# Four-layer graph network on one core: four-head attention weights that hold the target exponential, with key tiles added pairwise by DMA, and residual adds and moments on VectorE and ScalarE

## The chip, the cores and the metric

The kernel runs on one core of a Trainium2 chip. The metric is the device time of one execution in microseconds (us). Three executions of the kernel before took 4344.05 to 4347.82 us, with a median of 4347.32 us.

## What is computed

The input `x` holds 16 graphs of 1024 nodes with 256 features, and `adj` is one 1024 x 1024 adjacency matrix for all of them. Four layers follow one another, each with a residual around it: `x = x + layer(relu(layernorm(x)))`. Everything is float32.

- Layers 0 and 1 are graph attention with one head. `h = inp W`, the score of query i and key j is `leaky_relu(s_i + t_j)`, where `s = h a1` and `t = h a2`; scores off the graph are masked, softmax runs over j, and the result is `attention h`, followed by relu (layer 0) or elu (layer 1).
- Layer 2 is dot-product attention with 8 heads of 32 features, masked with `adj`, followed by a layer norm, a feed-forward block of two 256 x 256 products with relu, and a second layer norm.
- Layer 3 is graph attention with 4 heads of 64 features and elu.

The core of layer 3 in the reference:

```python
ei = jnp.einsum('bhnd,hd->bhn', Wh, a1)
ej = jnp.einsum('bhnd,hd->bhn', Wh, a2)
e = ei[:, :, :, None] + ej[:, :, None, :]
e = jnp.where(e > 0, e, ALPHA * e)
e = jnp.where(adj[None, None] > 0, e, MASK_VAL)
att = jax.nn.softmax(e, axis=-1)
h = jnp.einsum('bhij,bhjd->bhid', att, Wh)
```

The kernel never forms e. Up to factors of i, which softmax cancels, `exp(leaky_relu(s_i + t_j))` is `max(r_i, e_j) * z_j` with `r_i = exp((alpha-1) s_i)`, `e_j = exp((1-alpha) t_j)` and `z_j = exp(alpha t_j)`. The last one, `z_j`, is called the target exponential here.

## The kernel before

**Stages and order.** A stage is one layer of one graph. The list `order` interleaves them: in the middle of the run the cycle is layer 2 of graph b, layer 1 of graph b+1, layer 3 of graph b, layer 0 of graph b+2. A stage's keys lie on the 128 partitions in 8 tiles j of 128 keys; queries lie along the free dimension.

**The planner.** Every piece of work is an `op` with an engine, a cost, a rank and the ops it waits for; buffers are `Hold`s in `Ring`s that an op takes and others end. At build time `forward` plays all ops against these costs and writes the instructions of each engine in that order. The stored string `RANKS` gives each op's due time, so the order on all engines is fixed before the run. VectorE and GpSimd ops that both read two tiles are marked `tiles`; the planner doesn't let them overlap.

**Layer 3** (`pair_item`, `pair_weights`, `pair_out`). For each of two head pairs hp and each key tile j, VectorE makes a tile p of 128 keys x 2 heads x 1024 queries (1 MB) with two instructions of line 1391: `max(r, e) * mask`, where r is a broadcast row of 1024 queries that comes by DMA through DRAM (line 1281), e is a per-key scalar and mask is uint8. Two key tiles make a step. TensorE multiplies them with the values v (line 1425: 16 matmul calls with 32 columns of weights each, 32 instructions in the trace), and then with the target exponential, spread over 32 columns, which gives the softmax sums (line 1449: 8 calls, 16 instructions in the trace). The values v themselves were multiplied by the target exponential by VectorE when they left the projection (lines 1183 and 1202). After 4 steps the accumulators are copied out by ScalarE (line 1440), transposed, divided by the sums, and added into x.

**Layer 2** (`dot_item`). For each half n of the queries, each group g of 4 heads and each key tile j: scores on TensorE (line 1545), exp on ScalarE (line 1559), mask on VectorE (line 1567), product with the values (line 1576). For two key tiles in turn, GpSimd issues a DMA that adds the odd tile of weights into the even one (line 1593, 1 MB), and TensorE sums only the added tile, with the constant 0/1 matrix `pick` (line 1605).

**Layers 0 and 1** (`gat_item`). VectorE makes the weights (line 1318), TensorE multiplies (line 1335), `gat_out` scales and adds the residual.

**Way in.** `way_in` normalises a node tile for the next layer: `stats_of` runs bn_stats and bn_aggr on VectorE (lines 1030, 1031) and the power -1/2 on GpSimd (lines 1034, 1035). Residual adds of layer 0 (line 1361) and of layer 2 (line 1738), and the add after the attention of layer 2 (line 1658), run on GpSimd.

**Buffers.** The ring `m` has 11 buffers of 1 MB for p, pe, q, k, y and the broadcast rows of layer 3; PSUM has three double banks (`u`), of which a score op takes two.

Of the kernel before, what the change touches and what calls it, by code (L numbers as in the profile page):

```python
# [28 lines left out]
U8 = mybir.dt.uint8  # L29
# [18 lines left out]
    "##,#M5#IA#&O#H2#2l#M)#'c#Q(#H#$6p#MC#GP##q##c#%-#$X##s##0##U#$0#$,##P##X##Y##1#$-##{#$)#$]#$M#%I#$j#$N#%E#%K#%Y"  # L48
    "##%#%O#%}#&Y#&d#&l#&s#';#'B##W##9#oB##N##B#oP##Z##?##>##[##D#ny##a$7g##`##r##l#$##$$#$8#$*##u##z#$6#$=##}#$(#$;"
    "##b#$V$8-##_##y$8,##d##A$7y##g##o#$'#$u##2#$9#$7#$K#%*##*#$H##]#$.##3#$A##t##v#$E#$F#,;##x##6#$5$%$##'#Q.##T#K9"  # L50
    "#K.#(,#%W#'`#'U#$n#)s#'k#%U#(`##^#%7#$&#$%#$1#$2#$C#$G#$I#$L##<#$?#$[#$4##f#%@#%L#&2#$<#$Q##j#81##w#%D#%Z#%`#Nz"
    "#$Z#$`####$r#&1#%f#%k#$Y#$k#%4#>9#%A#%5#%r#%&#%M#${#%=#&##xD#%{#'u#%a#'q#(:#%z#'t#$i##h#$+#$d#$_#$h#$s#$e#$@#`+"
    "#%?#$>#&B#&%#,R#&Z#[=#%;#$O#$v##i##H#'H#%g#%J#%[#%0#%/#%,#&M$D{#$x#%>#%N#%h#b8$?s#&0#(3#&+#&.#%y#%u#&($4Z#&&#&6"
    "#%b#&$#&)#&'$B+#&_#))#&:#%p#Du#;z#<%#%V##n$H^#$b#$p$3b#$^#T>$3P#$m#%1##(#%T##O#%|##R#$}$GF##-#$U##4##8##K#%.##$"
    "##M#%:#$y#$t#$q##I#$z#%<#$W#%)#%8#=M#%6#%+##/##&##@#$g#$a#%w#-%#-##%R$&s##5$=J#%H#%]#3Q#%i#,V#/+#&5#$l#&h#:-#CG"
    "#:=#%d#$S#$|#%2#%c#%j#%m#&,#%t#$J#$w#%x$?=#%C#)*#%F#%B#%l#$o#&-#(U#%Q#'2#+6#%o#&/#0,$'e#'G#h`##p#0'#%^#&7$Gw##k"
    "#%v$Hv#&F$Ha#&N#'-#&A#&Q#&V#&S#lN#&m#&4#'3#'/#b##':#%q#&a#&*#(l#&w#&{#&z#&9#&<$Hw#%S#(R#y$#(S#'6#&;#&?#&^#lO#&G"
    "#Y}#'X#'0#&W#&I#%X#)D#(?#'+#R0#&[#&L#&P#'J#(+#&H#'1#&R#&|#',#'@#&p#'Q#'r#&k#'Y#&f#'C#(f#'.#'L#(8#(=#'N#&U#;v#;l"
    "$-[#&K#&=#&b#&E#&g#&j#&t#''#%s#&i#&o#(y#'9#(;#6F#(<#&n#'$#'8$H'#'a#'y$4|#'5#&]#')#'s#&}$Bt#'^$7k#'l#'?#'<$C2#'h"
    "#'K#'}#<K#%$#'o##.#(6##C#'W#%(#(%##e#'E#'4#'S#'m#'R#'I#(5#'w#'(#'>#'x#jJ#&y$=Z#<J$:z#'F#'O#'7#%G#{)#&v#'z#)V#>U"  # L60
    "#'n#'_#%n#(&#'p#?/#(0#'M#(.#&J#(/#'j#&`#rr#_c#(F#8j#(q#Mm#(M#Mo#(d#Mn#'&#'%#(##'Z#{g#(*#)a#&8##:#(2#(N#(E#/V#)I"
    "#(B#(A#(C#(4#)]$+r#,e#)M#([#i&#((#()#,t#i'#w/#)c#(t#I2#(J#(Y#]h#(K#(V#)F#(_#Ms#(u#KE$Ea#)-#(c#N+#)S#IC#)b#)`#)g"
    "#)U#(i#)d#*(#8?#(m#(|#).#jZ#)1#(a#)$#LT#)##(g#)u#jQ#)n#)0#*R#(k#)8#)@#)C#(j#(]#({#(@#)R#']#)E#(Z#(n#'{#'A#(^#)T"
    "#)>#)G#(P#)&#)5#)v#*&#'P#(G#(X#)y#'D#)L#*q#);#Lj#'|#(9#*3#*$#(D#*,#)K$I0#(O$I@$,q#*##)B#)i#*;#(H#*+#*4#+H#*E#)J"
    "#+L#*9#)A#s}#**#(1#+@#)O#)x#*7#*P#/`#*a#*A#*Z#*8#VE#)?#*D#*0#*y#*6#-0#)N#*_#*k#+k#*s#*C#*^#b($$C#)=#*c#)t#*v#J2"
    "#*[#(w#*w#+U#*I#*i#zG#'v$>>#B=#*]#*g$J:#,h$%D#W5#*n#*M#+<#*|$B<#++#*O#WG#+/#*J#.'#+G$J;#+M#+?#*f#z}#*t#a)#*r$?%"
    "#+A#+8#*j#*u$3:#*d#*p#+d#+a#*S#,U#+C#)+#*-#+`#)}#+&#*K#/?#+R#CO#+O#+P#*}#+[#*'$*M#+^#+S#-[#+X#+c#),#0>#)4#)9#,$"
    "#'*#,v#+N#,r#,W#-<#,N#[S#,x#,O#-:#+D#-A#-G#,B#,d#-(#,j#-;#,L#--#+z#-C#,z#'[#-6#,i#-D#/b#[@#-I#.^#-a$EU#.J#.%$;%"
    "#-}#+b#-j#g)#.:#.)$9j#.7#.?#+B#+F#-H#+(#,&#R+#,D#,%#^1#+#$(u$%|#+)#(Q#-Z#,|#)Y#Lh#*>#2n#+g#+J#*1#cw#)X#,T#+T#,g"
    "#.&#,y#,l#+3#*)#,Z#+e#(-#+>#cj#,'#(L#-2#,5#,)#g`#,6#,:#,4#+}#,##C(#,Q#($$1`#+Z#,9#,X$5H#*L#)W$1_#,Y#-s#,0#+o#,b"  # L70
    "#|5#*B#,}#+r#,s#,?#,@#,>#+u#,n#,8$5J$=r#,K#+]#-Q#+n#.,#-?#.;#,J#+j#+p$5Q#)P#.<$5K#,f#+i#,M#,G#)%#+{#,1#,H#rc#+l"
    "$5P#,3#,S#zA#):#,I$Ab#,c#,/$En#.4$02#*F#,`#,u#,7#-9#+V#-e#,*#-c#.=#-v#-^#-@#-o#-Y#+q#-3#-K#-n#-p#.I#+f#.H#JZ#kE"
    "#,m#.P#.U#,k#.T#-|#.o#/(#k3#.V#.Y#-r#.b#.d#/3#,[#.*#-U#.t#.g#.s#.]#/1#-E#.R#.w#.W#.v#.n#,P#+.#-L#,+#-h#ho#/f#/P"
    "#-5#.k#/O#,]#,-#/Q#0r#/K#/)#/^#8/#-t#8M#-x#-w#/W#-l#)f#(s#)l#)[#*l#+4#)m#*N#*m#)o#+'#%'#)e$<.#*.#)w#*:#*<$Eg$,p"
    "#it#*`#*T#(x#*b#*U#(z$GW#)r#*/#*%#)z#(I#*Y#){#,(#)Q#)|#+I#*e#(>#)Z#*V#*X#)<#*x#*h#W6#+%#+7#`p#+*#+5#`s#+-#+9#^*"
    "#+0$%f#*=#.N#-'#-&#-)#+y#-,#-1#,a#-/#-4#-7#-]#z6#-J$;&#,_#-f#-d#.D#-$#-P#&C$;5#+:#.6#+=#-`#-i#-q#.3#J[#/d#0y#0U"
    "#.M#rQ#B3#.@#-B#,o#.K#,{#0n#._#?V#-g#-z#/t#,.#.9#.e#.G#/Y#.E#.h#/>#-k#./#.L#-F#.+#.8#.A#-X#.C#/0#-=#-{#/'#8-#.["
# [281 lines left out]
    "$Fz$IH$J-$HT$Ib$79#Ul$I?$J5$I+$G|$Iu#hA$EL$Hp$HW$H?$GV$I/$.{$HD#`j$Ig$H_$H:$78#<0#V>$J.$Hs$Ho$Du$HG#GJ$I.$Hu$H|"  # L359
    "#1Z$3G$Hf$HS#_;$HL$Hg$IW#('#y'#<E#xi$I_$J*#M{$J#$I1$J1$GR$I|#<x$II$GO$I($IS#WD$IX$Ia$IV$I]$IB#UX#UW$IT$@<$Im$I="  # L360
    "#q^$IG$IU$IQ$Id$IO#^r$IM#>M$Iz$HI$2d$CB#>e$Iy#yW$It$I}#p4#TS$J?$0R#pU$IZ$Ie$Ij$HN$I:$J@$Hq$Hm$Ih$IP$IL$Ip$I$#:["
    "$I,$IN#5e$I'$If$IY#Y&$Hy#m_$J6#%P$J%#jY$Il#k;#al$J8#wr$I{$J'$J9$Ir$I>"
)


# [1585 lines left out]
```

## Time and profile before

| what | us |
|---|---|
| three executions, median | 4347.32 |
| the profiled execution, whole | 4346.76 |
| its span, first to last instruction | 4344.9 |
| TensorE matmuls busy in it | 4143.8 (95%) |
| VectorE busy | 3368.5 (78%) |
| ScalarE busy | 2004.2 (46%) |
| GpSimd busy | 1408.4 (32%) |
| queue of the adding DMAs, share of 16 DMA engines | 30.7% |

In the profile, PE is TensorE, PEld its weight loads, DVE is VectorE, ACT is ScalarE, POOL is GpSimd and SP issues most DMAs. A row of a group gives line, engine, operation, output and inputs, count, busy time and mean duration of one, and then the idle time just before, with what ended it. The busy time of a group can be less than count times mean, since consecutive instructions overlap a little.

### The profile page before, as it was taken

Reading aid. Unit: us, or ns where it says so; the run is one execution under the profiler, and the core shown is the slowest. Engines: PE = TensorE matmul, PEld = TensorE weight load, DVE = VectorE, ACT = ScalarE, POOL = GpSimd, SP = SyncE. Lnnn points to the kernel's source line nnn. Section 1 sums busy time; section 2 is a strip of 40 time slices with the busy share of each in tenths; the row PEclk is TensorE's granted clock in tenths of the full one; section 3 lists DMA queues with packets and bytes.
Section 4 is the critical chain, followed back from the end, with each engine's and each line's share of the span. In section 5 each row is a group of like instructions: output and inputs, shape, how many; then the busy total and the mean of one; then the engine's idle time right before and its main releaser. Section 6 shows DMA issues by size and latency. Waiting matters only on the chain. (4 is left out here: it accounts for less than half of the span.)

```text
span 4344.9 us, 66664 instructions
## 1 busy us (share of the span) xinstructions
PE 4143.8 (95%) x25993; PEld 2175.8 (50%) x25993; DVE 3368.5 (78%) x5836; ACT 2004.2 (46%) x3083; POOL 1408.4 (32%) x2281
## 2 busy tenths in 40 slices
PE   8999999998999999999999999998999999899988
PEld 7735264553645535455354554535545355464433
DVE  7578877878777788777878778777787877858788
ACT  4462635435354453634536354363543635455442
POOL 3323242423324233242322424224242241434231
PEclk9999999999999999999999999999999999999999
DMA  3061805317053170531606235162350713435261
GB/s 111 17 142 32 169 27 117 69 50 155 25 119 79 40 148 26 129 71 46 140 26 141 59 75 111 37 130 59 74 112 33 150 42 89 96 75 111 64 122 41
DMA packets 96451, 364.29 MB, mean 84 GB/s; under 512 B 10376, under 2 KB 45568, under 8 KB 63360
## 3 DMA queue, kind: packets, MB, share of 16 engines
q0 software_dynamic: 36864, 268.45, 30.7%
q1 hardware_dynamic: 58848, 90.98, 6.2%
q8 instruction: 206, 3.38, 0.3%
q14 instruction: 117, 0.96, 0.1%
q10 hardware_dynamic: 416, 0.52, 0.0%
HBM read 74.32 MB, written 17.17 MB: 21 GB/s over the span
## 5 line engine op out<-in xcount | busy, mean ns | idle before, releaser
L1567 DVE TENSOR_TENSOR pe<-pe,mask 128x1024 f32<-128x1024 f32 x1024 | 1206.9, 1233 | 190.5 <-ACT pe L1559 188.3
L1559 ACT ACTIVATE pe<-sc 128x1024 f32<-128x1024 f32 x1024 | 995.4, 1023 | 369.7 <-PE sc L1545 313.8
L1335 PE MATMUL av<-v,p 128*128 128x257 f32 x4096 | 966.8, 387 | 8.5 <-DVE p L1318 6.1
L1335 PEld LDWEIGHTS av<-v,p 128*128 128x128 f32 x4096 | 771.1, 192 | 202.2 <-issue 62.0
L1391 DVE SCALAR_TENSOR_TENSOR p<-r,e,mask 128x1024 f32<-128x1024 f32 x512 | 621.9, 1274 | 95.7 <-DMA r<-kept 85.8
L1545 PE MATMUL sc<-qT,kT 32*128 32x512 f32 x4096 | 626.3, 645 | 2.5 <-ACT pe L1559 2.5
L1035 POOL TENSOR_TENSOR rstd<-rstd,minus_half 128x1 f32<-128x1 f32 x768 | 565.5, 736 | 64.0
L1576 PE MATMUL acc<-pe,v 128*32 128x512 f32 x4096 | 543.0, 605 | 6.1 <-DVE pe L1567 4.7
L1593 POOL DMA_DIRECT2D pe<-pe x256 | 225.6, 888 | 976.8 <-PE acc L1576 669.5
L1034 POOL TENSOR_SCALAR rstd<-stats 128x1 f32<-128x1 f32 x768 | 281.8, 367 | 789.5 <-DVE stats L1031 765.3
L1425 PE MATMUL acc<-p,v 128*32 128x512 f32 x4096 | 465.9, 593 | 0.0
L1605 PE MATMUL sums<-pe,pick 128*32 128x512 f32 x2048 | 294.6, 637 | 127.2 <-DMA pe<-pe 126.4
L1545 PEld LDWEIGHTS sc<-qT,kT 32*128 32x128 f32 x4096 | 192.6, 184 | 388.8 <-issue 184.4
L1061 PE MATMUL pm<-l_wx,hT 128*128 128x259 f32 (+1 forms) x1536 | 369.5, 389 | 2.4 <-ACT hT L1057 1.4
L1318 DVE SCALAR_TENSOR_TENSOR p<-r,e,mask 128x512 f32<-128x512 f32 x512 | 359.2, 755 | 6.8 <-DMA r<-kept 6.4
L1061 PEld LDWEIGHTS pm<-l_wx,hT 128*128 128x128 f32 x1536 | 287.4, 191 | 73.1 <-ACT hT L1057 12.8
L1361 POOL TENSOR_TENSOR x<-x,o 128x256 f32<-128x256 f32 x128 | 100.6, 787 | 570.4 <-ACT o L1357 570.1
L1425 PEld LDWEIGHTS acc<-p,v 128*32 128x32 f32 x4096 | 132.1, 110 | 293.1 <-issue 277.4
L1576 PEld LDWEIGHTS acc<-pe,v 128*32 128x32 f32 x4096 | 100.6, 109 | 353.0 <-issue 223.9
L1030 DVE BATCH_NORM_STATS2 st<-x 128x6 f32<-128x256 f32 x512 | 212.4, 415 | 62.7 <-POOL x L1361 51.3
L1107 ACT ACTIVATE xn<-x,stats 128x256 f32<-128x256 f32 x256 | 124.7, 505 | 291.4 <-DVE stats L1031 235.1
L1449 PE MATMUL sums<-p,e 128*32 128x512 f32 x2048 | 247.5, 593 | 0.3 <-DVE p L1391 0.3
(106 smaller groups left out, 3920.5 us busy)
## 6 DMA issues: line engine op xcount, KB each, us to landing
pe<-pe POOLq DMA_DIRECT2D x256, 1024.0 KB, 8.1
r<-kept SPq DMA_DIRECT2D x64, 512.0 KB
x<-in_x_dram SPq DMA_DIRECT2D x32, 512.0 KB
out_dram<-x SPq DMA_DIRECT2D x64, 256.0 KB
r<-kept SPq DMA_DIRECT2D x62, 256.0 KB
edges<-in_adj_dram SPq DMA_DIRECT2D x8, 512.0 KB
kept<-rows_sb SPq DMA_DIRECT2D x128, 2.0 KB
qkv_sb<-in_L_gnn_w_qkv_dram SPq DMA_DIRECT2D x1, 768.0 KB
```

The source lines that it names most:

```text
L1034: nc.gpsimd.tensor_scalar(rh.t, mh.t[:, 1:2], EPS, None, ALU.add)
L1035: nc.gpsimd.tensor_tensor(rh.t, rh.t, minus_half, ALU.pow)
L1061: nc.tensor.matmul(dst, lhsT=lhsT[:, k, :], rhs=rhs[:, k, :], start=(k == 0), stop=(k == KC - 1))
L1318: nc.vector.scalar_tensor_tensor(ph.t[:, j % each, :], rh.t, s.e[:, j, H + h : H + h + 1], mask[:, j, cols], ALU.max, ALU.mult)
L1335: nc.tensor.matmul(avh.t[:, : s.hs + 1], lhsT=phs[part].t[:, j % each, i * P : (i + 1) * P], rhs=s.v[:, j, h, :], start=(j == 0), stop=(j ...
L1391: nc.vector.scalar_tensor_tensor(ph.t[:, hh, :], s.rh[hp].t[:, hh, :], s.e[:, j, col : col + 1], mask[:, j, :], ALU.max, ALU.mult)
L1425: nc.tensor.matmul(acc[n].t[(2 * hh + part) * W : (2 * hh + part + 1) * W, :], lhsT=s.v[:, jj, h, part * W : (part + 1) * W], rhs=p, start ...
L1545: nc.tensor.matmul(scs[pair].t[:, hh, :], lhsT=s.kh.t[r0 : r0 + D2, g, j * P : (j + 1) * P], rhs=s.qh.t[r0 : r0 + D2, g, cols], start=True ...
L1559: lambda pair=pair: nc.scalar.activation(part(pair), scs[pair].t, AF.Exp, scale=SCALE2),
L1567: lambda pair=pair: nc.vector.tensor_tensor(part(pair), part(pair), masks(), ALU.mult), [ex], tiles=True,
L1576: nc.tensor.matmul(head(acc, i), lhsT=s.v[:, j, g * QUAD + i, :D2], rhs=ph.t[:, i, :], start=(j == 0), stop=(j == NT - 1))
L1605: nc.tensor.matmul(head(sums, i), lhsT=pick[:, g, :], rhs=th.t[:, i, :], start=first, stop=last)
```

## The change

1. Layer 3 weights take the target exponential in. ScalarE writes mask times z_j into the tile (new op `scaled`, 512 instructions of 128 x 1024, uint8 to float32), and VectorE's instruction reads the tile itself in place of the mask. Values v are no longer multiplied by z_j: a ScalarE copy with the row's scale takes the place of VectorE's product.
2. With z_j inside, the sums need no weights of their own. The two tiles of a step are added by a DMA from GpSimd (new function `gather`, used by both attention layers), and TensorE sums the added tile with `pick`: 4 calls a step in place of 8. The base tile is held until its sum, the other until the DMA has landed.
3. The rows r of the second head pair are asked for only after the second values op of the first pair (`later_rows`). The fill of a tile waits for a values op two steps back (`paced`, AHEAD = 2).
4. Residual adds leave GpSimd for VectorE, and each writes its row sum as an accumulator. For layers 1, 2, 3 and for the last norm of layer 2, bn_stats and bn_aggr are replaced by `moments_of`: GpSimd turns the sum into a negative mean, ScalarE squares with it as a bias and accumulates, GpSimd makes the root.
5. The planner knows a sixth engine QUEUE, one adding DMA at a time, 5.2 long; `RANKS` holds a new plan. The ring `turned` is taken in order.

The core of the diff (the stored plan, the planner's bookkeeping for a sixth engine and repeated edits are left out):

```diff
-            if L in (0, 3):
+            if L == 3:
+                s.lead[t] = ex = op(
+                    ACT, 0.16, rank,
+                    lambda: nc.scalar.activation(s.e[:, t, :], pm()[:, C:width], AF.Exp, scale=rh.t),
+                    [vals, r_op], ends=[rh],
+                )
+                s.vops[t] = op(
+                    ACT, 0.37, rank + 0.6,
+                    lambda: nc.scalar.activation(s.v[:, t, :, : s.hs], heads(), AF.Copy, scale=rh.t),
+                    [ex], ends=[pmh, rh],
+                )
+                return
+            if L == 0:
...
+                def scaled(hh=hh, col=col):
+                    nc.scalar.activation(ph.t[:, hh, :], mask[:, j, :], AF.Copy, scale=s.e[:, j, col + H : col + H + 1])
+
                 def weights(hh=hh, col=col):
+                    part = ph.t[:, hh, :]
                     nc.vector.scalar_tensor_tensor(
-                        ph.t[:, hh, :], s.rh[hp].t[:, hh, :], s.e[:, j, col : col + 1], mask[:, j, :], ALU.max, ALU.mult
+                        part, s.rh[hp].t[:, hh, :], s.e[:, j, col : col + 1], part, ALU.max, ALU.mult
                     )
+                paced = s.value_ops[-AHEAD:][:1] if len(s.value_ops) >= AHEAD else []
+                filled = op(
+                    ACT, 0.95, first - 1.5 + 1.3 * hh, scaled, [s.rops[hp], s.lead[j]] + paced + (filled if hh else []),
+                    takes=[] if hh else [ph], ends=[s.eh],
+                )
...
             def totals():
-                both(lambda jj, n, hh, h, p: nc.tensor.matmul(
-                    sums.t[(2 * n + hh) * W : (2 * n + hh + 1) * W, 0, :],
-                    lhsT=s.e[:, jj, 2 * H + h : 2 * H + h + 1].to_broadcast([P, W]), rhs=p,
-                    start=(jj == 0), stop=(jj == NT - 1),
-                ))
+                for n in range(NH):
+                    for hh in range(2):
+                        nc.tensor.matmul(
+                            sums.t[(2 * n + hh) * W : (2 * n + hh + 1) * W, 0, :],
+                            lhsT=pick[:, 0, 0:1].to_broadcast([P, W]), rhs=th.t[:, hh, n * HALF : (n + 1) * HALF],
+                            start=(base == 0), stop=(j == NT - 1),
+                        )
...
+        def gather(th, ph, after, rank):
+            def start():
+                nc.gpsimd.dma_start(
+                    out=th.t.rearrange("p i q -> p (i q)"), in_=ph.t.rearrange("p i q -> p (i q)"), accum_op=ALU.add
+                )
+            issued = op(POOL, 0.9, rank, start, after, delay=0.6)
+            return op(QUEUE, 5.2, rank, lambda: None, [issued], ends=[ph])
...
-            gathered = op(POOL, 1.0, at[0] - 4.0, gather, [valued] + ready + masked, ends=[ph], delay=8.0)
+            s.gathered = [gather(th, ph, [valued] + ready + masked + s.gathered, at[0] - 4.0)]
...
+        def moments_of(src, scratch, mh, rank, after, shift=False, takes=(), ends=()):
+            rh = buffer(small, "rstd", (P, 1), "rstd")
+            def square():
+                nc.scalar.activation(scratch(), src(), AF.Square, bias=mh.t[:, 0:1], accum_out=mh.t[:, 1:2])
+            def root():
+                nc.gpsimd.tensor_scalar(rh.t, mh.t[:, 1:2], 1.0 / C, EPS, ALU.mult, ALU.add)
+                nc.gpsimd.tensor_tensor(rh.t, rh.t, minus_half, ALU.pow)
+                if shift:
+                    nc.gpsimd.tensor_scalar(mh.t[:, 1:2], mh.t[:, 0:1], rh.t, None, ALU.mult)
+            m_op = op(
+                POOL, 0.25, rank,
+                lambda: nc.gpsimd.tensor_scalar(mh.t[:, 0:1], mh.t[:, 2:3], -1.0 / C, None, ALU.mult), after,
+            )
+            q_op = op(ACT, 0.45, rank + 0.4, square, [m_op], takes=[rh, *takes], ends=ends)
...
-                add = op(POOL, 0.7, rank + 0.9, lambda: nc.gpsimd.tensor_add(xt(), xt(), oh.t), [o], ends=[oh], tiles=True)
+                add = op(
+                    DVE, 0.4, rank + 0.9,
+                    lambda: nc.vector.scalar_tensor_tensor(
+                        xt(), oh.t, 1.0, xt(), ALU.mult, ALU.add, accum_out=mh.t[:, 2:3]
+                    ), [o], takes=[mh], ends=[oh], tiles=True,
+                )
...
-                    nc.gpsimd.tensor_add(yt, yt, zh.t.rearrange("p (t c) -> p t c", t=TH))
+                    nc.vector.tensor_add(yt, yt, zh.t.rearrange("p (t c) -> p t c", t=TH))
...
-                    y2 = s.y[:, t : t + 2, :]
-                    nc.vector.tensor_add(y2, y2, pmh.t[:, u].rearrange("p (u c) -> p u c", u=2))
+                    for i, mh in enumerate(mhs):
+                        yt = s.y[:, t + i, :]
+                        nc.vector.scalar_tensor_tensor(
+                            yt, yt, 1.0, pmh.t[:, u, i * C : (i + 1) * C], ALU.mult, ALU.add, accum_out=mh.t[:, 2:3]
+                        )
```

In this last edit the PSUM tile of the second feed-forward product also serves as scratch for the squares, so it is held until four ScalarE squares are done.

## Prediction

> **What bounds the kernel now.** I read the busy table first, then TensorE's waits, then one middle cycle of four stages by stretch, then the order of time inside it.
>
> ```profile
> PE 4143.8 (95%) x25993; PEld 2175.8 (50%) x25993; DVE 3368.5 (78%) x5836; ACT 2004.2 (46%) x3083; POOL 1408.4 (32%) x2281
> ```
>
> TensorE is the bound: 201 us of the span are not matmul time. Its waits name the largest part of them:
>
> ```profile
> PE sums L1605 <- DMA pe<-pe: 126.4, 64, 6.7
> PE tp L1054 <- ACT xn L1107: 11.9, 5, 7.5
> PE pm L1061 <- ACT hT L1057: 11.0, 11, 1.2
> ```
>
> 64 of the 256 sums of layer 2 come to TensorE before their adding DMA has landed. By stretch (columns: window, length, busy PE, PEld, DVE, ACT, POOL, clock, DMA share, GB/s) the cycle of layer 2, layer 1, layer 3, layer 0 reads:
>
> ```profile
> 2046.00:2138.00 92.00, 90.12 (x651) 29.74 (x645) 81.76 (x100) 63.41 (x75) 26.99 (x38) 1.00 0.80 164
> 2138.00:2217.80 79.80, 73.74 (x329) 52.50 (x325) 59.79 (x146) 28.82 (x54) 35.79 (x70) 1.00 0.23 57
> 2217.80:2270.30 52.50, 52.50 (x446) 21.11 (x445) 45.78 (x70) 16.99 (x36) 11.31 (x17) 1.00 0.03 11
> 2270.30:2318.00 47.70, 47.70 (x263) 34.27 (x260) 29.17 (x56) 23.89 (x37) 14.91 (x26) 1.00 0.25 69
> ```
>
> The third line is layer 3: TensorE has no gap, but VectorE is at 87% beside it, ScalarE at 32%, the DMAs idle. So layer 3 can give TensorE time back only until VectorE's 45.8 us are reached. Its steps in order of time on TensorE, and VectorE's start:
>
> ```profile
> 2217.85 3.64 PE L1425 MATMUL acc<-p,v 128*32 128x512 f32 x32
> 2221.31 1.90 PE L1449 MATMUL sums<-p,e 128*32 128x512 f32 x16
> 2223.03 3.62 PE L1425 MATMUL acc<-p,v 128*32 128x512 f32 x32
> ...
> 2206.95 14.44 DVE L1391 SCALAR_TENSOR_TENSOR p<-r,e,mask 128x1024 f32<-128x1024 f32 x12 [6.19 <-DMA r<-kept]
> ```
>
> Start to start, values take 3.45 us and sums 1.72. The weights can't begin before the rows r land.
>
> **What the Trainium skill says.** "VectorE: DVE Perf Modes", section on the TRN2 errata, prices a ScalarE instruction from SBUF at 224 cycles plus the elements, at 1.2 GHz: 1.04 us for 1024. The trace has 0.625 for 512 (L1506), where the page gives 0.613; it agrees. "DMA: Bandwidth & Descriptors", on the anatomy of a GpSimd DMA, gives 2.0 us plus bytes over 436 GB/s, so 4.4 us for 1 MB; the trace has 8.1 us to landing for the adding DMA, and 30.7% of 4344.9 us over 256 is 5.2 us of all engines each. The measurement decides. The same page's section on issuing engines says that DMAs of all queues share the 16 engines; that matters for the row loads. "SBUF — State Buffer", on who interferes with whom, says that a VectorE instruction with two SBUF inputs and a GpSimd instruction that reads SBUF exclude each other. The masks of L1567 have a minimum of 1160 ns, a median of 1218 and a maximum of 3206, which fits but doesn't show the cause.
>
> **The change, part by part** (against the profiled execution, 4346.8 us; the median lies 0.6 above it).
>
> *Sums of layer 3.* Removed: 128 groups of 16 matmul instructions at 1.72 us, 220.2. Added: 128 groups of 8, each as the groups of L1605, 0.88 start to start, 112.6. TensorE: -108, all on the path, if something else doesn't become late.
>
> *Adding DMAs and their waits.* 128 more issues on GpSimd at 0.888 (L1593), 114 us beside other work; 128 x 5.2 = 666 us of DMA time where the share was 0.03. A sum waits if TensorE has too little work between the last product that frees the DMA and the sum. I added trace durations along TensorE's order in both built programs. In layer 2, 67 of 256 gathers had under 7 us before and 47 now; what is missing to 8.1 us adds up to 217.7 us before and 195.6 now. Before, this stood for 126.4 us of measured waits, 0.58 of it. So layer 2 gives back 22.1 x 0.58 = 13 and the new ones, missing 44.3, cost 26: +13. From below: were the waits to fall as the count under 7 does, layer 2 would give 38.
>
> *The fill on ScalarE.* 512 new instructions. No row shows one from uint8 in SBUF with a per-key scale. From 1.012 (L1142, PSUM, 1024), plus 0.039 for SBUF (0.625 against 0.586 for 512), plus 0.099 for a per-partition operand (L1703 0.685 against L1615 0.586): 1.15 us, some 1.05 where they follow closely. Bounds 0.97 and 1.25. They could cost the end nothing only where ScalarE is idle, so I look at layer 3 alone. In the built order, a typical stage has on ScalarE, from first to last fill, 32 fills and 15 us of other work: 48.7. Time for it: from the row transpose (L1250) to the first values op TensorE has 16.7 us of work, from there to the end of the last values op 45.9 (50.0 before), and the rows take 8.8 us from the transpose to the first weight (2198.15 to 2206.95): 53.8. The last weight (1.2) and half a values op (1.7) come after the last fill, so 50.9 is left; ScalarE has 2.2 us of slack. VectorE, with the same 50.7 us of rows by mean durations in both programs, lost 6.3 us in waits between 2206.95 and 2260.2. If ScalarE loses as much, the stage grows by 4.1 us; if its waits fit, by 0. I take 1.75: 14 stages, +25. The bounds are 0 and 14 x (4.1 + 32 x 0.1) = 102.
>
> *The last two stages* have no other layer to fill gaps: the step becomes VectorE's 4 x 1.215 (621.9 over 512) = 4.86 against 5.17, so a pair gains 0.31 and not 0.84: 16 x 0.53, +9.
>
> *What the fill waits for.* A fill stands in ScalarE's order behind a landing DMA (base or odd tile must come free), then VectorE and TensorE wait for it; behind it stand the normalising and evacuating instructions of the next layer 0 and the copies of L1440 that free the accumulator. With six tiles in use, the loop over three steps is landing 8.1, fill 1.1, four weights 4.9, values 3.45: 17.6, or 5.9 a step, against 45.9 / 8 = 5.7 that TensorE's order gives. As three steps are filled ahead, I cost this at nothing; if that cover goes, it is the slower rival. The gathers wait on GpSimd for a values op; behind them stand means and roots, for which ScalarE and VectorE wait. The later rows are two 512 KB loads on SP behind a TensorE op; x loads and stores stand behind them, none due within a stage.
>
> *Residual adds and moments.* VectorE loses L1202 (52.4), 128 of L1183 (28.7), and 384 + 128 bn pairs (159 + 52 + 512 x 0.182 = 305): 386. It gains 256 adds at 0.477 (L1373), 128 PSUM adds at 0.46 in place of 41.9, 64 adds at 0.73, and 512 accumulator reads at 0.080 (as after L689): 122 + 17 + 47 + 41 = 227. Net -159 of 3368, beside TensorE: 0. ScalarE gains 512 squares at 0.505 (L1107), 259, and 128 copies at 0.473, 61; its accumulator read isn't shown, 0 to 0.1 each. GpSimd loses 306 (L1361, L1738, L1658) and gains 512 x 0.36 = 184 and the issues, about -8. The chain to a norm is a ScalarE and a GpSimd step longer, 0.9 us, and the feed-forward tile holds one of three double banks for about 2 us longer while scores want two. I cost both at 0; shorter adds (0.73 for 1.41 in L1658) lie against them. Bounds -20 and +35.
>
> Sum: -108 + 13 + 25 + 9 = -61; 4346.8 - 61 + 0.6 = **4286**.
>
> **Rivals.**
> - *TensorE stays the bound and the new plan spaces the sums better.* For it: the third stretch has DMAs and ScalarE idle; fewer gathers stand close. Against: VectorE and ScalarE above 93% in layer 3. -108 - 13: 4226.
> - *No change: the saved time becomes waiting in layer 3.* ScalarE loses in waits what VectorE lost, so a stage grows by 4.1 us, and a fill takes 1.12 and not 1.05, 2.2 us more over 32: 14 x 6.3 = 88. -108 + 13 + 88 + 9 = +2: 4349. For it: two engines above 90% that wait for each other in turn. Against: VectorE alone was as full before, and TensorE had no gap.
> - *Slower: the loop over the tiles.* In layer 3 the fill of step k+3 waits for the landing of step k. If landings take 13 us (17.8 is the longest seen in layer 2, and 1 MB of rows now loads beside them), the loop is 22.5 / 3 = 7.5 a step; five steps of a stage lose 1.8, 9 us, 14 stages 126 instead of 25: 4387. It decides from a landing of about 10 us on.
> - That the change doesn't do what it says can be left out: the built order has 512 sums calls where there were 1024.
>
> **How the numbers follow.** Forecast 0.45, clean gain 0.18, no change 0.15, slower 0.22. A measurement of this kernel can't tell less than 0.2% (8.7 us) from nothing. Faster: 0.45 + 0.18 + 0.06 of the third; same 0.07; slower 0.24. The range goes from 4205, inside the clean case, to 4375, inside the slower one; the forecast's own is 4250 to 4335.
>
> **What would show it.** TensorE's layer 3 sums at some 125 us busy in 1024 instructions; the fill near 1.1 us; waits of sums for DMAs near 110 and 26 us; in a middle stretch of layer 3 ScalarE above 90%, the step between 5 and 6 us. I am wrong if values ops wait more than 5 us a stage for weights (too many waits), if landings exceed 10 us (the loop), or if scores wait for banks in layer 2.

## The result, and the profile after

The changed kernel takes 4316.5 us (median of four executions, 4310.1 to 4323.6) and the kernel before 4345.9 beside it: a ratio of 0.9933, 95% interval 0.9916 to 0.9950. That is 29 us faster, where the forecast was 61. The profiled execution took 4317.4 us with a span of 4315.3.

Busy time first (page of the changed kernel; busy us, share, instructions):

```profile
PE 4071.8 (94%) x24969; PEld 2134.7 (49%) x24969; DVE 3140.0 (73%) x5452; ACT 2836.9 (66%) x4747; POOL 1354.0 (31%) x2601
```

TensorE is busy 72 us less, and its idle time grew from 201.1 to 243.5, by 42. The difference, 30, is the gain. The removed sums alone were worth more than 72, so something also got longer. The groups show it (busy, mean ns | idle before, releaser). Single matmuls overlap a good deal, not a little as it says ahead of the prediction: 32 of them with a mean of 593 ns take 3.6 us together, so the busy time of a group is far below count times mean.

```profile
L1480 ACT ACTIVATE p<-mask,e 128x1024 f32<-128x1024 uint8 x512 | 555.5, 1143 | 49.7 <-PE sums L1565 33.2
L1525 PE MATMUL acc<-p,v 128*32 128x512 f32 x4096 | 499.2, 618 | 25.7 <-DVE p L1484 25.5
L1565 PE MATMUL sums<-p,pick 128*32 128x512 f32 x1024 | 145.3, 617 | 33.7 <-DMA p<-p 32.0 <-DVE rows_sb L1329 1.4 <-ACT v L1279 0.3
```

Layer 3's sums went from 247.5 to 145.3, -102. But its values, the same 4096 instructions, went from 465.9 to 499.2, +33; the last section shows why. TensorE's waits (us in total, times, longest):

```profile
PE sums L1728 <- DMA pe<-pe: 35.0, 43, 4.5
PE sums L1565 <- DMA p<-p: 32.0, 20, 4.0
PE av L1416 <- DVE p L1399: 26.7, 8, 6.1
PE tp L1118 <- ACT xn L1179: 26.0, 13, 7.5
PE acc L1525 <- DVE p L1484: 25.5, 13, 7.6
```

The first was 126.4 before: layer 2 gave back 91 us. The third was 6.1, the fourth 11.9, and the second and fifth are new. By stretch, the cycle of layers 2, 1, 3 and 0 that answers to the one in the prediction (same columns):

```profile
2055.60:2151.00 95.40, 91.53 (x656) 29.67 (x654) 81.91 (x105) 60.21 (x77) 21.87 (x31) 1.00 0.89 182
2151.00:2221.80 70.80, 65.45 (x287) 51.07 (x287) 34.84 (x105) 44.70 (x108) 31.56 (x85) 0.95 0.05 16
2221.80:2280.60 58.80, 52.76 (x383) 23.03 (x382) 44.68 (x62) 45.92 (x65) 19.20 (x25) 1.00 0.74 157
2280.60:2325.50 44.90, 44.90 (x228) 31.89 (x228) 33.30 (x62) 24.35 (x46) 9.00 (x18) 0.96 0.23 65
```

Layer 3, the third line, is longer than before, 58.8 us for 52.5, though TensorE has 8.5 us less of sums in it (15.2 to 6.7). Of what is more, 7.4 us are other work: the new order has put products of layer 2's projection into this stretch, which had none of them before. This is one of two such lines:

```profile
2225.61 3.70 PE L1125 MATMUL pm<-hT,qkv_sb 128*128 128x512 f32 x8
```

The rest of it is idle time. No engine is full: VectorE 76%, ScalarE 78%, TensorE idle for 6.0 us. The DMA share went from 0.03 to 0.74. Counting the gaps of all twelve middle layer-3 stages in the trace, from their first values to the first layer-0 values, TensorE idles 77.7 us where it idled 0.0: 35.1 before layer 0's values, 17.0 before sums, 15.6 before transposes of xn, 6.2 before layer 3's values.

The end of that stage shows the largest of these. TensorE, then the row DMAs on SP's queue, then VectorE, each from the timeline of the changed kernel (start, length, what; idle before and releaser in brackets):

```profile
2268.30 7.37 PE L1525 MATMUL acc<-p,v 128*32 128x512 f32 x64
2275.17 1.36 PE L1565 MATMUL sums<-p,pick 128*32 128x512 f32 x8
2280.59 4.78 PE L1416 MATMUL av<-v,p 128*128 128x257 f32 x13 [4.06 <-DVE p L1399]
```
```profile
2267.39 0.65 SPq L1337 DMA_DIRECT2D kept<-rows_sb  x1
2272.61 2.10 SPq L1351 DMA_DIRECT2D r<-kept  x2
```
```profile
2279.69 2.74 DVE L1399 SCALAR_TENSOR_TENSOR p<-r,e,mask 128x512 f32<-128x512 f32 x4 [4.93 <-DMA r<-kept]
```

The row of layer 0 goes to DRAM at 2267.39, its loads can start only at 2272.61, and the first weight at 2279.69: 12.3 us. Before, the same three points took 6.2 us, with the values 9 us after the first weight. Now they follow it by 0.90.

```profile
2255.48 0.65 SPq L1262 DMA_DIRECT2D kept<-rows_sb  x1
2257.43 0.80 SPq L1276 DMA_DIRECT2D r<-kept  x2
2261.71 10.68 DVE L1318 SCALAR_TENSOR_TENSOR p<-r,e,mask 128x512 f32<-128x512 f32 x16
```

So it is in eight of the twelve middle stages, with 11.3 to 14.0 us; in the other four the chain takes about 6, and before it took 4.9 to 8.9. The store and the loads that wait for it stand among 1 MB adding DMAs, which land after 8 to 9 us (median):

```profile
pe<-pe POOLq DMA_DIRECT2D x256, 1024.0 KB, 8.3
p<-p POOLq DMA_DIRECT2D x128, 1024.0 KB, 8.7
```

The gain also shrinks at the end. When the last stretch of layer-3 values begins, the changed kernel is 62 us ahead (4165.5 against 4227.8). From there to the end it takes 149.8 us, where it took 117.1. The last sums have nothing in front of them to hide a landing:

```profile
4282.22 3.64 PE L1525 MATMUL acc<-p,v 128*32 128x512 f32 x32
4286.43 1.06 PE L1565 MATMUL sums<-p,pick 128*32 128x512 f32 x8 [0.58 <-DMA p<-p]
...
4291.43 1.94 PE L1565 MATMUL sums<-p,pick 128*32 128x512 f32 x8 [2.91 <-DMA p<-p]
4296.81 1.94 PE L1565 MATMUL sums<-p,pick 128*32 128x512 f32 x8 [3.44 <-DMA p<-p]
```

Values end at 4285.9, sums at 4298.8. Before, the last sums were done ahead of the last values. With direct sums (below) the same last part takes 131.2 us, so some 19 of the 33 us more come with the adding DMAs. TensorE waits 8.2 us in it for their landings and 11.4 for weights, 7.6 of these at 4243.86, behind loads of rows that took 10.5.

### The profile page after: what moved, and what is told of

Read it like the earlier page. It is cut to its first block, busy times and chain, and to the rows that moved or that the text cites. A ratio compares the mean times of both kernels' runs of the same rounds, so it can differ in the third digit from the quotient of the medians.

```text
span 4315.3 us, 66211 instructions
## 1 busy us (share of the span) xinstructions
PE 4071.8 (94%) x24969; PEld 2134.7 (49%) x24969; DVE 3140.0 (73%) x5452; ACT 2836.9 (66%) x4747; POOL 1354.0 (31%) x2601
## 5 line engine op out<-in xcount | busy, mean ns | idle before, releaser
L1416 PE MATMUL av<-v,p 128*128 128x257 f32 x4096 | 974.2, 388 | 53.4 <-DVE p L1399 26.7
L1484 DVE SCALAR_TENSOR_TENSOR p<-r,e,p 128x1024 f32<-128x1024 f32 x512 | 631.4, 1278 | 229.1 <-ACT p L1480 203.0
L1480 ACT ACTIVATE p<-mask,e 128x1024 f32<-128x1024 uint8 x512 | 555.5, 1143 | 49.7 <-PE sums L1565 33.2
L1525 PE MATMUL acc<-p,v 128*32 128x512 f32 x4096 | 499.2, 618 | 25.7 <-DVE p L1484 25.5
L1101 POOL TENSOR_SCALAR stats<-stats 128x1 f32<-128x1 f32 x512 | 167.9, 337 | 705.5 <-DVE x L1445 452.0
L1095 POOL TENSOR_TENSOR rstd<-rstd,minus_half 128x1 f32<-128x1 f32 x512 | 332.0, 648 | 42.6
L1728 PE MATMUL sums<-pe,pick 128*32 128x512 f32 x2048 | 269.2, 603 | 35.5 <-DMA pe<-pe 35.0
L1653 POOL DMA_DIRECT2D p<-p x128 | 116.0, 911 | 500.1 <-PE acc L1525 451.0
L1094 POOL TENSOR_SCALAR rstd<-stats 128x1 f32<-128x1 f32 x512 | 161.3, 315 | 319.7 <-ACT xn L1091 150.4
L1439 ACT ACTIVATE o<-av,inv 128x256 f32<-128x256 f32 x256 | 120.2, 470 | 184.2 <-DVE inv L1433 183.7
```

The costliest lines, as they stand in the source:

```text
L1095: nc.gpsimd.tensor_tensor(rh.t, rh.t, minus_half, ALU.pow)
L1416: nc.tensor.matmul(avh.t[:, : s.hs + 1], lhsT=phs[part].t[:, j % each, i * P : (i + 1) * P], rhs=s.v[:, j, h, :], start=(j == 0), stop=(j ...
L1480: nc.scalar.activation(ph.t[:, hh, :], mask[:, j, :], AF.Copy, scale=s.e[:, j, col + H : col + H + 1])
L1484: nc.vector.scalar_tensor_tensor(part, s.rh[hp].t[:, hh, :], s.e[:, j, col : col + 1], part, ALU.max, ALU.mult)
L1525: nc.tensor.matmul(acc[n].t[(2 * hh + part) * W : (2 * hh + part + 1) * W, :], lhsT=s.v[:, jj, h, part * W : (part + 1) * W], rhs=p, start ...
L1653: nc.gpsimd.dma_start(out=th.t.rearrange("p i q -> p (i q)"), in_=ph.t.rearrange("p i q -> p (i q)"), accum_op=ALU.add)
```

## The experiments

Theory A: the traffic of layer 3's adding DMAs gives back what the shorter sums save, through late rows and long landings. Theory B: ScalarE, with fills and squares, is too full. Theory C: the 91 us of layer 2 come from the plan, whose `forward` now plays the queue, and not from lighter engines. The first four kernels and the one with half adds keep the changed kernel's order of instructions. For the others, where ops or costs change, `RANKS` was searched again with the kernel's own `forward`. The two controls change nothing but the result of such a search. The record has one such order for each kernel. Every ratio is to the kernel before, at 4343.9 to 4348.8 us beside them.

**Layer 3's adding DMAs made tiny.** Each moves 16 numbers a partition in place of 2048, so layer 3's sums lack nearly all of the odd tiles.

```diff
-        def gather(th, ph, after, rank):
+        def gather(th, ph, after, rank, width=2048):
...
-                    out=th.t.rearrange("p i q -> p (i q)"), in_=ph.t.rearrange("p i q -> p (i q)"), accum_op=ALU.add
+                    out=th.t.rearrange("p i q -> p (i q)")[:, :width],
+                    in_=ph.t.rearrange("p i q -> p (i q)")[:, :width], accum_op=ALU.add
...
-                    gather(th, s.p[hp, jj], s.base + s.gathered + [s.pops[hp, jj, hh] for hh in range(2)], at[0])
+                    gather(th, s.p[hp, jj], s.base + s.gathered + [s.pops[hp, jj, hh] for hh in range(2)], at[0], 16)
```

> The changed kernel with its order of instructions kept, but each adding DMA of layer 3 moves 64 bytes a partition in place of 8 KB, so layer 3's sums are not what they should be. Theory A (the traffic of the new adding DMAs is what eats the gain: rows of the layer-0 stage land 12 us after their store and not 5, sums and fills wait for landings): the 1 MB DMAs cost the sums' waits (32 us), the late rows (about 40) and part of the late weights (20 to 60), so the time falls by 80 to 130, to about 4190 to 4240; store to first layer-0 weight goes back to 5 to 6 us. Theory B (ScalarE is too full: fills and squares come late whatever the DMAs do): only the sums' waits go, 32 us, to about 4285.

Measured: 4225.8 us, ratio 0.9723 (0.9705 to 0.9742), 91 us below the changed kernel. The wait of sums for p is gone from the list, and so are the late rows: TensorE is idle for 2.8 us before layer 0's values in the twelve stages, where it was 35.1. Between the two traces TensorE's idle time falls by 65 us (243.5 to 178.5), and its busy time by 27 for the same instructions (4071.8 to 4044.4), beside a mean granted clock of 0.988 in place of 0.981. So the adding DMAs cost both gaps and slower matmuls. Theory A; B's number is missed by 60.

**No fills.**

```diff
-                    nc.scalar.activation(ph.t[:, hh, :], mask[:, j, :], AF.Copy, scale=s.e[:, j, col + H : col + H + 1])
+                    pass
...
-                        part, s.rh[hp].t[:, hh, :], s.e[:, j, col : col + 1], part, ALU.max, ALU.mult
+                        part, s.rh[hp].t[:, hh, :], s.e[:, j, col : col + 1], mask[:, j, :], ALU.max, ALU.mult
```

> The changed kernel with its order kept, but without the 512 fills: VectorE takes the mask itself, so the weights lack the target's exponential. Theory B (ScalarE too full): values no longer wait for weights (about 58 us) and ScalarE's other results come earlier (transposes and products of the next layer wait 25 us less), so the time falls by 60 to 90, to 4225 to 4255. Theory A (DMA traffic): the weights are earlier, but tiles still come free only after landings and the rows are as late as before: it falls by 10 to 40, to 4275 to 4305.

Measured: 4313.0 us, ratio 0.9933 (0.9916 to 0.9949): the same as with the fills, though ScalarE is busy 524 us less. Theory B is out; theory A's number, 10 to 40 less, is missed too. The waits of this kernel say where the time stays:

```profile
PE sums L1565 <- DMA p<-p: 53.8, 23, 5.1
PE av L1416 <- DVE p L1399: 33.7, 9, 5.2
PE acc L1525 <- DVE p L1484: 17.1, 8, 7.2
PE tp L1118 <- ACT xn L1179: 9.5, 3, 7.4
```

The values of layer 3 and the xn transposes wait 25 us less (25.5 and 26.0 in the changed kernel), and the sums and the values of layer 0 wait 29 us more (32.0 and 26.7 there).

**Short squares.**

```diff
-                nc.scalar.activation(scratch(), src(), AF.Square, bias=mh.t[:, 0:1], accum_out=mh.t[:, 1:2])
+                nc.scalar.activation(scratch()[:, :32], src()[:, :32], AF.Square, bias=mh.t[:, 0:1], accum_out=mh.t[:, 1:2])
...
-                nc.gpsimd.tensor_scalar(rh.t, mh.t[:, 1:2], 1.0 / C, EPS, ALU.mult, ALU.add)
+                nc.gpsimd.tensor_scalar(rh.t, mh.t[:, 1:2], 1.0 / 32, EPS, ALU.mult, ALU.add)
```

> The changed kernel with its order kept, but the 512 squares on ScalarE take 32 of 256 columns (the variance is that of 32 columns), about 0.19 us each less, 95 us of ScalarE in all; the accumulator reads stay. Theory B (ScalarE too full): part of the late xn, hT and weights goes, 20 to 40 us, to about 4275 to 4295. Theory A: the squares lie beside TensorE, 0 to 10 us.

Measured: 4314.8 us, ratio 0.9929 (0.9913 to 0.9946). Nothing; the squares lie beside TensorE.

**Rows of layer 0 already in DRAM.** The core of the edit:

```diff
+                if s.layer == 0 and s.b > 1:
+                    kept.append(fixed[0])
+                    return
...
```

> The changed kernel with its order kept, but layer-0 stages from batch 2 on store no rows and load those of batch 1, which lie in DRAM long since, so the output is not right. It takes one of two DMAs in a row out of the way from transpose to weights. Theory A says that what makes layer 0 begin late is the two DMAs queued among the adding DMAs of layer 3: store to first weight was 12 us in most stages and falls to about 6, the waits of layer-0 values for weights (35 us in 12 stages) go, so the time falls by 25 to 40, to about 4275 to 4290. If the rows are late because ScalarE or VectorE bring the transpose late, the time falls by less than 10.

Measured: 4286.3 us, ratio 0.9873 (0.9856 to 0.9889), 30 us below the changed kernel. Layer 0's values wait 1.4 us for their weights in place of 26.7, while sums wait 42.5 us for their landings. So the late rows alone cost 30 us, in an order that is otherwise the same.

**The queue in the plan of the kernel before, and that kernel only searched again.** The first, whose planner also gets the sixth engine and takes the ring `turned` in order, as in the change:

```diff
-            gathered = op(POOL, 1.0, at[0] - 4.0, gather, [valued] + ready + masked, ends=[ph], delay=8.0)
+            issued = op(POOL, 0.9, at[0] - 4.0, gather, [valued] + ready + masked, delay=0.6)
+            gathered = op(QUEUE, 5.2, at[0] - 4.0, lambda: None, [issued], ends=[ph])
...
```

> The kernel before with one part of the change alone: its planner knows the DMA queue of layer 2's adding DMAs (0.9 us issue, then 5.2 us on the queue, 1.4 us to landing; the turned tiles in order) and the order was searched again. No adds, squares or fills are moved. Theory C (the 91 us of layer-2 waits that vanished are the plan's doing): layer-2 sums wait for DMAs 30 to 60 us in place of 126, time 4255 to 4295. If they vanished because VectorE and GpSimd have less to do, the waits stay near 100 and the time is 4320 to 4350.

> The kernel before with nothing but its order searched again under its own planner, which doesn't know the queue; the control of the kernel with the queue in the plan (4268.6), with as much effort. If the queue model made the gain, the sums of layer 2 still wait about 100 to 130 us and the time is 4320 to 4350; if more searching made it, 4260 to 4290.

Measured: 4268.6 us, ratio 0.9820 (0.9804 to 0.9837), with the queue in the plan; 4352.8 us, ratio 1.0021 (1.0014 to 1.0028), without it. The wait for layer 2's landings, in the first and in the second:

```profile
PE sums L1613 <- DMA pe<-pe: 57.7, 51, 6.4
```
```profile
PE sums L1605 <- DMA pe<-pe: 140.5, 79, 4.7
```

Theory C: searching alone brings nothing, the queue in the plan (with `turned` in order) brings 84 us, and no engine's work has changed.

**Direct sums in layer 3.** The adding DMAs are taken out, and `totals` multiplies both tiles by `pick` again; all else of the change stays:

```diff
-            for jj in tiles[base in tiles :]:
-                s.gathered = [
-                    gather(th, s.p[hp, jj], s.base + s.gathered + [s.pops[hp, jj, hh] for hh in range(2)], at[0])
-                ]
...
-                PE, 0.8575, at[0] + 6.0, totals, s.gathered + ([] if first else [s.last_sums]),
-                takes=[sums] if first else [], ends=[th], form=32,
+                PE, 1.715, at[0], totals, weights + ([] if first else [s.last_sums]),
+                takes=[sums] if first else [], ends=held, form=32,
...
```

> The changed kernel with one part undone: layer 3's sums multiply both tiles (16 instructions a step, 1.72 us), no adding DMA in layer 3; all else of the change stays, and the order was searched again. Theory A (the traffic of layer 3's adding DMAs eats nearly all that the shorter sums give): time 4290 to 4335, the rows of layer 0 land 5 to 6 us after their store, TensorE has under 3 us of gaps in a middle layer-3 stage. If the adding DMAs are a net gain of the size of the removed sums, it is slower than the changed kernel by 60 to 110: 4375 to 4425.

Measured: 4220.3 us, ratio 0.9707 (0.9690 to 0.9723). This is 96 us faster than the changed kernel and 70 below the range that theory A had expected. Its busy line, its longest wait and a middle layer-3 stage:

```profile
PE 4095.1 (97%) x25993; PEld 2157.2 (51%) x25993; DVE 3137.7 (74%) x5452; ACT 2839.5 (67%) x4747; POOL 1234.1 (29%) x2473
```
```profile
PE sums L1714 <- DMA pe<-pe: 44.7, 49, 2.4
```
```profile
2162.50:2218.70 56.20, 56.14 (x455) 22.75 (x454) 47.37 (x71) 44.08 (x63) 11.38 (x17) 1.00 0.03 10
```

TensorE has 1024 instructions more than in the changed kernel, is busy only 23 us more, though its sums in layer 3 take 101 us more (246.2 for 145.3), and idle 122 us less. The granted clock is 0.995 where it was 0.981. In the stage of layer 3 shown it has no gap beside nearly the same ScalarE load (44.1 us for 45.9).

**The rows' delay in the plan, and the control.**

```diff
-                        delay=4.0 if H == 1 else 6.0,
+                        delay=(10.5 if s.layer == 0 else 4.0) if H == 1 else 6.0,
```

> The changed kernel with one number of its planner changed: the rows of a layer-0 stage come 10.5 us after their load is issued and not 4.0 (store to first weight measured 12 to 13 us with layer 3's adding DMAs in flight), and the order searched again with the same effort as in the next kernel. Nothing is computed differently. Theory A: the transposes are put earlier, layer-0 values wait under 10 us in all for their weights, 20 to 40 us faster than the next kernel. If the rows' lateness only stands in for another limit, it is the same within 10.

> The changed kernel with only its order searched again, the planner's costs unchanged, as the control of the kernel before it and of the one with direct sums. Every theory: within 20 us of the changed kernel, 4295 to 4335, since the planner still takes rows for earlier and squares and fills for shorter than they are.

Measured: 4268.1 us, ratio 0.9819 (0.9803 to 0.9836), against 4303.0, ratio 0.9887 (0.9870 to 0.9905), for the control. Layer 0's values wait 0.8 us for weights, in the control 30.4. The 35 us agree with the 30 of the rows that were ready. The control gives a first scale for a new search: 13 us below the stored order.

**Half adds.** As the tiny ones, with another width:

```diff
-                    gather(th, s.p[hp, jj], s.base + s.gathered + [s.pops[hp, jj, hh] for hh in range(2)], at[0], 16)
+                    gather(th, s.p[hp, jj], s.base + s.gathered + [s.pops[hp, jj, hh] for hh in range(2)], at[0], 1024)
```

> The changed kernel with its order kept, and layer 3's adding DMAs half as large: 4 KB a partition in place of 8 (the sums lack half of the odd tiles). 64 bytes gave 4226, 8 KB give 4316. If the loss goes with the bytes moved, 4266 to 4276. If it comes from landings that exceed what the order leaves (about 6 us to the sum, rows 12 us after the store), a landing near 5.5 us is already short enough, and most of the 90 us is back: 4230 to 4250.

Measured: 4225.5 us, ratio 0.9721 (0.9705 to 0.9737), the same as with 64 bytes. Their landing, from the page:

```profile
p<-p POOLq DMA_DIRECT2D x128, 512.0 KB, 4.6
```

So the loss doesn't go with the bytes. A landing of 4.6 us fits into the order, one of 8.7 (over 10 in 38 of 128 cases) doesn't. Where between them the limit lies, and whether it is the length of a landing or how long the queue is taken, two sizes don't tell.

**Adding DMAs for the first pair of heads only.** The second pair has direct sums as above:

```diff
-            for jj in tiles[base in tiles :]:
+            for jj in tiles[base in tiles :] if hp == 0 else ():
...
-                PE, 0.8575, at[0] + 6.0, totals, s.gathered + ([] if first else [s.last_sums]),
+                PE, 1.715 if hp else 0.8575, at[0] + 6.0, totals,
+                (weights if hp else s.gathered) + ([] if first else [s.last_sums]),
...
```

> The changed kernel with adding DMAs only for the first pair of heads of each layer-3 stage, the second pair's sums direct, order searched again: 54 us less TensorE work than the kernel with direct sums (4220), none of the new DMAs near the rows of layer 0 or the end of the stage. Theory A in its stricter form (the loss is the collision with the rows and the next stage) gives 4180 to 4215. If each adding DMA of layer 3 costs its share wherever it stands (tiles held for a landing in a ring of 11), it lies between 4220 and 4303, at 4245 to 4275.

Measured: 4251.4 us, ratio 0.9777 (0.9761 to 0.9794): 31 us above direct sums with half of the DMAs, where all of them cost 83 (4303.0). The stricter form of theory A, that only the collision at the end of the stage costs, has missed its range by 36.

**Direct sums with measured costs.** The adds with sums get theirs as well:

```diff
-                    ACT, 0.95, first - 1.5 + 1.3 * hh, scaled, [s.rops[hp], s.lead[j]] + paced + (filled if hh else []),
+                    ACT, 1.05, first - 1.5 + 1.3 * hh, scaled, [s.rops[hp], s.lead[j]] + paced + (filled if hh else []),
-            q_op = op(ACT, 0.45, rank + 0.4, square, [m_op], takes=[rh, *takes], ends=ends)
+            q_op = op(ACT, 0.62, rank + 0.4, square, [m_op], takes=[rh, *takes], ends=ends)
...
```

> Direct sums in layer 3, and the planner's costs as measured: fill 1.05 (0.95), square 0.62 with its accumulator read (0.45), the adds with sums 0.5 and 1.0 (0.4 and 0.8); order searched again. If ScalarE's mis-stated costs make xn, hT and the weights late, 10 to 30 us faster than 4220; if ScalarE has room enough, within 10 of it.

Measured: 4202.8 us, ratio 0.9669 (0.9652 to 0.9685), the fastest version that leaves nothing out: 142 us below the kernel before, 17.6 below direct sums. Whether the truer costs did it isn't shown: a search alone moved the control by 13.

**Half adds that the plan knows.**

```diff
-            return op(QUEUE, 5.2, rank, lambda: None, [issued], ends=[ph])
+            return op(QUEUE, 5.2 if width == 2048 else 2.6, rank, lambda: None, [issued], ends=[ph])
```

> Layer 3's adding DMAs move half the columns (the sums lack half of the odd tiles), as in the kernel with half adds (4225), and the planner knows it (2.6 us on the queue) and searched again. With direct sums the kernel takes 4220 though its TensorE has 110 us more to do. If it is only the order, spaced out for 8 us landings, that keeps the 110 us from showing, this one takes 4120 to 4150. If layer 3 is held by its weights (ScalarE, then VectorE, 4.9 us a step) whatever the DMAs do, it stays above 4190.

Measured: 4198.4 us, ratio 0.9660 (0.9644 to 0.9676). The number lies in the branch "held by its weights", but the waits don't say that:

```profile
PE sums L1729 <- DMA pe<-pe: 40.0, 36, 4.2
PE sums L1565 <- DMA p<-p: 17.4, 15, 4.3
PE acc L1525 <- DVE p L1484: 7.9, 6, 2.5
```

Layer 3's values wait 7.9 us for weights in the whole run. Against direct sums, 104 us of sums are gone from TensorE in the trace (224.2 to 120.3, overlaps counted once), its busy time fell by 66 only, and its idle time rose from 122 to 168, over many small waits. The granted clock is 0.990 in place of 0.995. Neither branch holds: even a cheap landing leaves 22 of the 104.

**The whole change with all measured costs in the plan.** The diffs of the rows' delay and of the measured costs together, on the changed kernel:

```diff
-                        delay=4.0 if H == 1 else 6.0,
+                        delay=(10.5 if s.layer == 0 else 4.0) if H == 1 else 6.0,
...
-            q_op = op(ACT, 0.45, rank + 0.4, square, [m_op], takes=[rh, *takes], ends=ends)
+            q_op = op(ACT, 0.62, rank + 0.4, square, [m_op], takes=[rh, *takes], ends=ends)
...
```

> The changed kernel whole, with everything that the runs showed put into its planner: rows of layer 0 at 10.5 us, fill 1.05, square 0.62, the adds with sums 0.5 and 1.0; order searched again. Nothing is computed differently. If the loss is what the planner didn't know, it comes down to the kernel with direct sums and measured costs (4203) or below. If 1 MB landings cost more than the shorter sums give even in a plan that knows them, it stays at 4240 to 4270.

Measured: 4305.1 us, ratio 0.9902 (0.9885 to 0.9919), above both numbers. Rows are no longer late, but the time is in the landings:

```profile
PE sums L1565 <- DMA p<-p: 66.4, 29, 5.4
```

A plan that knows the rows and the costs doesn't rescue the adding DMAs of layer 3. It is 37 us above the kernel with the rows' delay alone (4268.1), which knows less: so plans differ by more than the 13 us of the control, and a difference of that size between two searched kernels is no proof by itself. With the rows' delay in the plan, the adding DMAs cost 48 against direct sums; with the planner's old costs in both, 83 (4303.0 against 4220.3); with all measured costs in both, 102 (4305.1 against 4202.8). They cost more than they bring in each of the three.

## Why the prediction was wrong, and what of it was right

By the terms of its sum:

| term | forecast | measured |
|---|---|---|
| sums of layer 3 | -108 | -102 busy |
| waits for landings in layer 2 | -13 | -91 |
| waits of the new sums for landings | +26 | +32 |
| fill on ScalarE | +25 | 0 (without fills: 4313 for 4316) |
| last two stages | +9 | +33 from the last stretch of values to the end; +14 with direct sums |
| what the fill waits for, rows, loads | 0 | +91 (tiny adds); rows are 30 of it, and the 32 above are in it |
| adds and moments | 0 | about -50 with fills and later rows, not separated |

The measured column doesn't add up to -29, because 102 us less work on TensorE are not 102 us less time. That the sums would take some 100 us less was right within 6. That they are "all on the path, if something else doesn't become late" was not: with tiny adds, which have the shorter sums and hardly any traffic, the kernel takes 4225.8 us, and with direct sums 4220.3; the best case with landings of 4.6 us gains 22.

**The step that failed is the one that put what the adding DMAs make late at nothing**: "As three steps are filled ahead, I cost this at nothing". What they make late measured 91 us, against 102 of saved work: by the two traces, 32 are the waits of the sums themselves, which had been forecast (26), another 32 the gaps before layer 0's values (35.1 to 2.8; 30 us of time with the rows ready), and 27 longer matmuls, for which the sum had no term. The DMAs that the text did look at beside them were x loads and stores, "none due within a stage"; the rows of layer 0 aren't among them. It had noted that DMAs of all queues share the 16 engines and that this matters for the row loads, and then gave it no number. The rows of layer 0 are a chain of two small DMAs, due at the end of just the stage into which the new DMAs were put. The stage before hid 6.2 us of it with 9 us to spare; 12.3 us left no cover. The slower rival, to which I gave 0.22, came nearest: it let long landings decide, and the half adds show that a short one costs no more than a tiny one. But the limit lies somewhere between landings of 4.6 and 8.7 us and not at about 10, and its path was the loop over the tiles, in which values wait for weights. These waits are only 25.5 us in the whole run. That its price, 126 us over 14 stages, is of the size of the 91 found is luck in part.

**The fill** was mis-sized: +25 forecast, nothing found. ScalarE is busy for 45.9 of 58.8 us in a middle stage, and taking 512 fills out changes nothing there, where the landings hold the stage; with direct sums and all fills TensorE has no gap in the stage of layer 3 shown. "ScalarE has 2.2 us of slack" counted the stage as long as TensorE's work; with landings in it the stage was longer than that. That the values got 33 us longer isn't a wait for weights either; see the last section.

**Layer 2** went wrong the other way. "0.58 of it" scaled a count of missing microseconds from the built orders, which came out at 217.7 and 195.6, nearly equal. The waits fell from 126.4 to 35.0. The missing time was counted to one landing of 8.1 us for each DMA alone; what a plan with a queue in it avoids is one landing waiting behind another. That my count lacked the queue is argued, not shown: landings over 12 us in layer 2 fell from 25 of 256 in the kernel before to 17 with the queue in its plan and to 4 in the changed kernel, while the waits fell from 126.4 to 57.7 and 35.0. That the plan did it is shown by 4268.6 against 4352.8.

So two wrong terms hid each other, and that the forecast had the right sign was luck in part. Put together from kernels with orders searched alike: the queue in the plan 84 us (4352.8 to 4268.6), the adds, moments, fills and later rows 48 more (to 4220.3), the adding DMAs of layer 3 83 the other way (to 4303.0). The change is faster than the kernel before because of its planner and, in smaller part, its other moves, and in spite of the adding DMAs of layer 3. The 48 us are beyond the bound of -20 that I set for adds and moments; some of it may be the search, and I didn't take it apart.

Open: why 82 of 104 us don't appear even when the landings are short. Of them 46 are new gaps, spread over several waits, and 38 longer matmul time, beside the lower granted clock; no one of them was isolated. The changed kernel's waits of xn transposes (26.0 us) come from the fills at least in part: in the timeline a fill that waits for a tile stands ahead of xn on ScalarE, and without fills they are 9.5 us, though the whole doesn't get shorter. A larger ring of tiles wasn't tried.

## What to carry to other kernels

Before you move work from a full engine to DMAs, list the small DMAs that are due in the same stretch, above all chains of two, and give each of their landings a number: here each link of the chain shown grew by some 3 us (store to load 1.95 to 5.22, load to first weight 4.28 to 7.08). Compare the landing with the time that the order leaves between issue and use, not the bytes with the bandwidth: half the bytes cost nothing here, the whole ones 91 us. And if a change brings a new order along, run the new order without the change: the two can have opposite signs.

## What was not expected of the hardware

In these traces TensorE often pays for a gap twice. After it, matmuls run at 1064 ns in place of 592 for some 3 us. From the timeline of the changed kernel, and then a stretch in it with its granted clock, 0.50 (third number from the end):

```profile
1965.82 0.44 PE L1118 MATMUL tp<-ident,xn 128*128 128x128 f32 x2 [1.91 <-ACT xn L1179]
1966.19 5.34 PE L1525 MATMUL acc<-p,v 128*32 128x512 f32 x32
```
```profile
1966.91:1970.31 3.40, 3.40 (x20) 0.87 (x16) 1.80 (x2) 2.82 (x3) 0.81 (x1) 0.50 1.02 212
```

The same 32 instructions take 3.6 us elsewhere. In ten traces, of both kernels and of all experiments up to the control of the rows' delay but the kernel before searched again, I took the gaps of 0.4 us and more that are followed by at least four matmuls of 128 rows and 512 columns between 1.3 and 3 us after their end, and called them slow when the median of these was above 900 ns. Of gaps under 1.2 us, 14 of 395 were followed by the slow form; from 1.2 to 1.6 us, 6 of 68; from 1.6 to 2.4 us, 41 of 105; above 2.4 us, 48 of 60. Several of these kernels share an order, so the counts aren't independent. The Trainium skill has the effect in "TensorE: Matmul & The Clock Gate", section on HAM oscillation, for gaps above about 3.4 us; here shorter ones are enough in many cases. The +33 us of layer 3's values go with it: 186 of their 4096 instructions ran slow, after gaps of 1.8 to 7.6 us, where the kernel before had none. In layer 2, where the waits went away, the mean of a sums instruction fell from 637 to 603 ns. So the slow spells moved with the gaps, and over the whole run the mean granted clock is about the same before (0.983) and after the change (0.981); with direct sums, where TensorE idles for 121.5 us and not 243.5, it is 0.995.

A store of 2 KB and the loads that follow it took twice as long beside the adding DMAs. The Trainium skill's "DMA: Bandwidth & Descriptors", section on issuing engines, says that the queues share the engines. From store to first weight it is 5 to 9 us in the middle stages of the kernel before and 5 to 8 with tiny adds; with the 1 MB adds it is 11 to 14 in eight of twelve stages.

An accumulator read on ScalarE after each square takes 0.19 us (mean 189 ns for those that follow xn), which the prediction had put between 0 and 0.1.
